# Second projections of a decoder layer: own values of kv heads 0 and 1 first, context values of these heads made between the others

## The chip, the cores and the metric

The kernel runs on one core of a Trainium2 chip. Its time is the device time of one execution in microseconds (us), given as the median of several runs. The kernel before takes 2528.96 us (three runs, 2527.68 to 2529.01). The engines are named as in the profile: PE is the matrix engine (PEld its weight loads), DVE the vector engine, ACT the scalar engine, POOL the GpSimd engine, and SP the queue that issues the DMAs.

## What is computed

One decoder layer, in float32, on x of 8 sequences x 100 tokens x 1024 and a context of 8 x 722 x 1024. Each of the three parts is added to its input and followed by a layer norm:

```python
x = layernorm(x + retention(x))                     # 8 heads, decay matrix, gate
x = layernorm(x + cross_and_self_attention(x, ctx)) # 16 query heads, 4 kv heads of 128
x = layernorm(x + swiglu(x))                        # 1024 -> 4096 -> 1024
```

The change is in the second part:

```python
q, k, v = x @ wq, x @ wk, x @ wv           # q: 16 heads, k and v: 4 heads ("own" keys and values)
q, k = rope(rms_norm(q, qw)), rope(rms_norm(k, kw))
k_ctx, v_ctx = rms_norm(ctx @ wk_ctx, kw), ctx @ wv_ctx
k_full, v_full = concat(k_ctx, k), concat(v_ctx, v)      # 722 + 100 rows
out = softmax(q @ k_full.T / sqrt(128) + mask) @ v_full  # per head
y = out @ wo
```

## The kernel before

**Arithmetic.** All large products are made from operands split in a high and a low part, so each 128x128 block of a product is three matmuls (`mm3`, lines 86, 87, 88). A weight block of 1024x128 is loaded by `load_w` (line 76) into one of three `wst` buffers and split by ACT (line 67) and DVE (line 68) into one of four `w` buffers. Context weights have been split earlier and are read whole by `load_ws` (line 82). `proj` makes one product of a weight block with 400 tokens (one half of the batch) or with half of a context: 24 matmuls into one PSUM bank. Banks are handed out in turn under three tags: three of "a", four of "s", one of "v". A bank is free for its next use when ACT and DVE have read it.

**Order.** The program is written stage by stage, but the instructions of each engine are put in an order by a scheduler that goes by its own estimate of when things become ready. Each engine works its own list strictly in that order. SP's list of DMAs is in order too: a DMA that waits holds those behind it. Tiles lie in pools; when a pool is closed its memory is used again by the next pool, and an instruction that writes there waits for the last reader of the tiles that lay there (`reuse_waits="tile"`).

**The stages around the change.**

1. `out_proj` (line 239 adds the residual) and the layer norm end the first part. They leave the normed activations in four tiles `z`, two for each half of the batch.
2. *Second projections* (pool "l2"). For each kv head there are six blocks: four query heads, one own key, one own value. Each block is made for both halves of the batch, so there are 48 "half-blocks". A query or key half-block takes the squares (ACT), a sum over partitions on POOL (line 125), the rotation (lines 133 to 137), an inverse root (lines 113 to 120), the scaling (line 645), a split, and a store to DRAM. A value half-block is only copied, transposed on PE (line 148), split into the single buffer `vs` and stored (line 637). Blocks come in groups: the four queries of kv head 0, its key and value, and then two by two. The context of the first sequence is loaded beside them, and the context keys of kv heads 0 and 1 (`context_keys`) are made between groups.
3. *Attention* (pools "cx" and "c1"), for 8 sequences x 4 kv heads, which are called heads below. Each makes context keys (unless made before) and context values (`context_values`, line 613), transposes the values (line 677), takes seven blocks of scores (lines 707, 711, 712), the maximum over partitions (line 125), the exponentials (line 730), their sum (line 733), the product with the values into the "v" bank, and the division by the sum (lines 747 to 752). The result goes through `ofs` and the split pair `oh` to DRAM (line 755).
4. `out_proj` of the second part, with the pool "y2" for its sum `y` and residual `rs`. Its first group makes four blocks at once: three in the "a" banks and one in an "s" bank, 48 matmuls each. The fifth block takes the first "a" bank again.

In the kernel before, pool "y2" is opened ahead of the attention, so its memory is apart from that of "cx" and "c1".

Of the kernel before, what the change touches and what calls it, by code (L numbers as in the profile page):

```python
# [16 lines left out]
P = 128  # L17
B, T, D = 8, 100, 1024
NB = 4
# [20 lines left out]
def decoder_layer(ctx, tc, xT, cT, w1, wo1, w2, wo2, wc, w3, wd, gw, qw, kw, trig, dec, mask, out):  # L40
# [15 lines left out]
    def f32(ap):  # L56
        return ap.bitcast(F32)
# [8 lines left out]
    def split2(hi, lo, src):  # L66
        nc.scalar.copy(hi, src)  # L67
        nc.vector.tensor_tensor(lo, src, f32(hi), ALU.subtract)  # L68

    def load_w(src, w=None, parts=1):  # L70
        st = wp.tile([P, KT * P], F32, tag="wst", name="wst", bufs=3)
        if w is None:
            w = wp.tile([P, 2, KT * P], FR, tag="w", name="w", bufs=4)
        for i in range(parts):
            c = slice(i * KT * P // parts, (i + 1) * KT * P // parts)
            nc.sync.dma_start(out=st[:, c], in_=src[:, c])
            split(w[:, :, c], st[:, c])
        return w
# [17 lines left out]
    def acc_tag():  # L96
        turn[0] += 1
        return "as"[turn[0] % 2]

    def proj(w, z, n=N, tag="a"):  # L100
        acc = bank(tag)[:, :n]
        for k in range(KT):
            t = z[k // QT]
            mmw(acc, w, k, t[:, 0, k % QT, :n], t[:, 1, k % QT, :n], k == 0, k == KT - 1)
        return acc
# [4 lines left out]
    def inv_root(pool, ss, eps, n=N, pin=False):  # L110

        r = pool.tile([P, n], F32, tag="r0", name="r0")
        ln = nc.scalar.activation(r, ss, AF.Ln, bias=eps)
        if pin:
            tc.keep_in_program_order(ln)
        nc.scalar.activation(r, r, AF.Exp, scale=-0.5)
        q = pool.tile([P, n], F32, tag="r1", name="r1")
        nc.scalar.activation(q, r, AF.Square)  # L118
        nc.vector.scalar_tensor_tensor(q, ss, eps, q, ALU.add, ALU.mult)  # L119
        nc.vector.scalar_tensor_tensor(q, q, 3.0, r, ALU.subtract, ALU.mult)  # L120
        return q

    def all_red(pool, x, tag, op=RED.add):
        y = pool.tile([P, N], F32, tag=tag, name=tag)
        nc.gpsimd.partition_all_reduce(y, x, P, op)  # L125
        return y

    def rope(pool, acc, cosw, sinw, tag="t1", op=ALU.add):

        t1 = pool.tile([P, N], F32, tag=tag, name=tag)  # L130
        t2 = pool.tile([P, N], F32, tag="t2", name="t2")
        h = P // 2
        nc.scalar.copy(t2[0:h], acc[h:P])
        nc.scalar.copy(t2[h:P], acc[0:h])
        nc.vector.tensor_tensor(bt(t1), bt(acc), cosw[:, None, :].to_broadcast([P, NB, T]), ALU.mult)
        nc.vector.tensor_tensor(bt(t2), bt(t2), sinw[:, None, :].to_broadcast([P, NB, T]), ALU.mult)
        nc.vector.tensor_tensor(t1, t1, t2, op)
        return t1

    def tokens_first(pool, acc, copied=True):  # L140

        vt = acc
        if copied:
            vt = pool.tile([P, N], F32, tag="vt", name="vt", bufs=1)
            nc.scalar.copy(vt, acc)
        tr = bank("s")
        for b in range(NB):
            nc.tensor.transpose(tr[0:T, b * P:(b + 1) * P], vt[:, b * T:(b + 1) * T], ident)  # L148
        return tr[0:T]
# [424 lines left out]
    def load_context(b):  # L574

        cz.clear()
        for hf in range(2):
            n = SN[hf]
            z = [big([P, 2, QT, SH]) for _ in range(2)]
            for k in range(0, KT, 2):  # L580
                cs = wp.tile([P, KT * P], F32, tag="wst", name="cs", bufs=3)
                cs = cs[:, :2 * n].rearrange("p (k n) -> p k n", k=2)
                nc.sync.dma_start(out=cs, in_=cT[b, :, k:k + 2, hf * SH:hf * SH + n])
                split(z[k // QT][:, :, k % QT:k % QT + 2, :n], cs)
            cz.append(z)

    def context_keys(kv):

        kall = ka.tile([P, 2, SC + T], FR, tag="kall", name="kall")
        wk = load_ws(2 * kv)  # L590
        sq = ka.tile([P, SC], F32, tag="ksq", name="ksq", bufs=1)
        ss = ka.tile([P, 6 * P], F32, tag="kss", name="kss", bufs=1)
        row = dr.tile([6, P], F32, tag="row", name="row", bufs=2)
        nc.gpsimd.memset(ss[:, SC:], 1.0)

        def step(hf):
            n, at = SN[hf], slice(hf * SH, hf * SH + SN[hf])
            acc = proj(wk, cz[hf], n)
            nc.scalar.activation(sq[:, at], acc, AF.Square)  # L599
            nc.gpsimd.partition_all_reduce(ss[:, at], sq[:, at], P, RED.add)  # L600
            nc.scalar.activation(kall[:, 0, at], acc, AF.Copy, scale=kws)
            nc.vector.scalar_tensor_tensor(kall[:, 1, at], acc, kws, f32(kall[:, 0, at]), ALU.mult, ALU.subtract)
            if hf:
                nc.sync.dma_start(out=row.rearrange("c p -> (c p)")[None, :], in_=ss[0:1])
        return step, (kall, row)

    def context_values(kv):

        wv = load_ws(2 * kv + 1)
        vt = ka.tile([P, SC], F32, bufs=1, tag="cvt", name="cvt")  # L610
        for hf in range(2):
            copy = nc.scalar.copy if hf == 0 else nc.vector.tensor_copy
            copy(vt[:, hf * SH:hf * SH + SN[hf]], proj(wv, cz[hf], SN[hf]))
        return vt


    early = []
    with sbuf("l2", 2) as p:
        for kv in range(NKV):
            for i0, i1 in ((0, 4), (4, 6)) if kv == 0 else ((0, 2), (2, 4), (4, 6)):  # L620
                if (kv, i0) == (0, 4):
                    load_context(0)
                ws = [load_w(w2[kv, i]) for i in range(i0, i1)]
                if (kv, i0) in ((1, 2), (2, 2)):
                    step, kept = context_keys(kv - 1)
                    early.append(kept)
                if (kv, i0) in ((1, 2), (2, 0), (2, 2), (3, 0)):
                    step(i0 == 0)
                for half in range(2):
                    bs = slice(half * NB, (half + 1) * NB)  # L630
                    for i in range(i0, i1):
                        acc = proj(ws[i - i0], z1[half], tag=acc_tag())
                        if i == 5:
                            tr = tokens_first(p, acc).rearrange("p (b d) -> p b d", b=NB)
                            vs = p.tile([T, NB, 2, P], FR, tag="vs", name="vs", bufs=1)
                            split2(vs[:, :, 0], vs[:, :, 1], tr)
                            nc.sync.dma_start(out=f32(vd[kv, :, bs]), in_=f32(vs))
                            continue
                        sq = p.tile([P, N], F32, tag="sq", name="sq")
                        nc.scalar.activation(sq, acc, AF.Square)  # L640
                        ss = all_red(p, sq, "ss")
                        tb = tq if i < 4 else tk
                        t = rope(p, acc, tb[:, 0], tb[:, 1])
                        r = inv_root(p, ss, eps_k)
                        nc.vector.scalar_tensor_tensor(
                            t, t, -0.5 if i < 4 else -0.5 * math.sqrt(P), r, ALU.mult, ALU.mult)
                        d = p.tile([P, NB, 2, T], FR, tag="d", name="d", bufs=3)
                        split2(d[:, :, 0], d[:, :, 1], bt(t))
                        nc.sync.dma_start(out=f32(qd[kv, i, :, bs] if i < 4 else kd[kv, :, bs]), in_=f32(d))
    z1pool.__exit__(None, None, None)  # L650


    y2pool = sbuf("y2", 1)
    y2p = y2pool.__enter__()
    with sbuf("cx", 2) as p, sbuf("c1", 1) as p1:
        for b in range(B):
            if b > 0:
                load_context(b)
            for kv in range(NKV):
                if early:  # L660
                    kall, row = early.pop(0)
                else:
                    step, (kall, row) = context_keys(kv)
                    step(0)
                    step(1)
                nc.sync.dma_start(out=f32(kall[:, :, SC:]), in_=f32(kd[kv, :, b]))
                vall = p.tile([P, NC, 2, P], FR, tag="vall", name="vall")
                nc.sync.dma_start(out=f32(vall[C5:P, 5]), in_=f32(vd[kv, 0:P - C5, b]))
# [1 line left out]
                q = p.tile([P, 4, 2, T], FR, tag="q", name="q")  # L670
                nc.sync.dma_start(out=f32(q).rearrange("p h l t -> p h (l t)"),
                                  in_=f32(qd[kv, :, :, b]).rearrange("h p l t -> p h (l t)"))
                vt = context_values(kv)
                for c0, c1, rows in ((0, 3, P), (3, 5, P), (5, 6, C5)):
                    tr = bank("s")
                    for c in range(c0, c1):
# [91 lines left out]

    fp = ctx.enter_context(sbuf("fp", 1, "right"))
    z2p = ctx.enter_context(sbuf("z2", 1, "right"))
    zb = {}
# [273 lines left out]
```

## Time and profile before

| | |
|---|---|
| median of three runs | 2528.96 us |
| the profiled execution, its own time | 2527.58 us |
| its span, first to last instruction | 2525.8 us |
| mean granted PE clock | 0.994 of full speed |
| busy: PE, DVE, ACT, POOL | 98%, 79%, 54%, 18% of the span |
| second projections, up to the last own value | about 590 to 841 us of the span |
| attention | about 849 to 1642 us |

What is worked out from single rows belongs to the profiled execution of 2527.58 us, which lies 1.38 us under the median. A row of the grouped view reads: line, engine, operation, output<-inputs, shape, count | busy time, mean length of one in ns | idle time of the engine just before it, and what ended that. A row of the waits reads: the waiting engine, output and line <- what it waited for: total us, times, longest. A window row reads: from:to, length, and for each engine busy us (number of instructions), then the granted PE clock, the DMA share, and GB/s.

### The profile page before, as it was taken

To read this page: it belongs to the slowest core of one execution; us is meant where nothing else is said; L and a number is where in the kernel's file an instruction comes from. 1 tells how busy PE (TensorE), PEld (TensorE's weight loads), DVE (VectorE), ACT (ScalarE), POOL (GpSimd) and SP (SyncE) were. 2 spreads that over 40 slices of the span, in tenths; PEclk is the share of its full clock that TensorE was granted. 3 is DMA by queue.
4 is the path that set the end of the run, shared out by engine and by line. 5 is a ranking of instruction groups with operands and counts; after the bars stand their busy time and mean duration, and the time that the engine had idled before them with its cause. 6 is when DMAs were issued, how large, how long until landed. Compare 5 with 4: busy or idle time off the path is not lost.

```text
span 2525.8 us, 37215 instructions
## 1 busy us (share of the span) xinstructions
PE 2478.2 (98%) x14042; PEld 2440.9 (97%) x14042; DVE 2000.6 (79%) x3106; ACT 1353.7 (54%) x2272; POOL 466.8 (18%) x230
## 2 busy tenths in 40 slices
PE   8999999999999999999999999999999999999997
PEld 8999999998899999999999999999999999998996
DVE  7778876568989798998998998866988777666756
ACT  6666676336667466655656566533554454432222
POOL 0111111002555243433433434100000000000000
PEclk9999999999999999999999999999999999999999
DMA  7333445774444654455554554575455445388742
GB/s 239 110 110 127 136 146 186 240 268 147 143 147 147 202 174 156 151 170 161 163 165 146 163 190 125 199 259 162 137 183 195 163 158 167 127 298 313 249 135 86
DMA packets 232898, 438.16 MB, mean 173 GB/s; under 512 B 47594, under 2 KB 176490, under 8 KB 220302
## 3 DMA queue, kind: packets, MB, share of 16 engines
q1 hardware_dynamic: 231566, 431.59, 51.3%
q0 software_dynamic: 1152, 4.19, 1.1%
q8 instruction: 110, 1.80, 0.3%
q14 instruction: 70, 0.57, 0.1%
HBM read 326.38 MB, written 109.35 MB: 173 GB/s over the span
## 4 chain that ended last, share of the span: by engine, by line
PE 89%; DVE 6%; issue 2%; DMA 1%; ACT 1%; SPq 0%; DVEq 0%; ACTq 0%
PE a L88 18%; PE a L86 18%; PE a L87 17%; PE s L88 9%; PE s L87 9%; PE s L86 9%; PE v L86 2%; PE v L88 2%; PE v L87 2%; PE s L486 1%; PE s L677 1%; DVE r L120 1%; DVE r L119 1%; PE s L148 1%; DVE d L68 1%
## 5 line engine op out<-in xcount | busy, mean ns | idle before, releaser
L86 PE MATMUL a<-big,w 128*128 128x400 f32 (+2 forms) x1824 | 616.3, 339 | 10.5 <-ACT big L67 7.1
L87 PE MATMUL a<-big,w 128*128 128x400 f32 (+2 forms) x1824 | 615.7, 338 | 0.0
L88 PE MATMUL a<-big,w 128*128 128x400 f32 (+2 forms) x1824 | 614.4, 338 | 0.0
L67 ACT CAST w<-wst 128x1024 fp32r<-128x1024 f32 (+1 forms) x243 | 251.8, 1039 | 431.0 <-PE s L88 152.3
L68 DVE TENSOR_TENSOR w<-wst,w 128x1024 fp32r<-128x1024 f32 (+1 forms) x243 | 297.7, 1227 | 120.2 <-ACT w L67 119.0
L86 PEld LDWEIGHTS a<-big,w 128*128 128x128 f32 x1824 | 343.7, 189 | 12.3 <-ACT big L67 7.4
L87 PEld LDWEIGHTS a<-big,w 128*128 128x128 f32 x1824 | 344.5, 189 | 1.4 <-DVE big L68 0.3
L88 PEld LDWEIGHTS a<-big,w 128*128 128x128 f32 x1824 | 344.2, 189 | 1.0 <-DVE w L68 0.3
L86 PE MATMUL s<-big,w 128*128 128x400 f32 x680 | 236.0, 347 | 0.1
L87 PE MATMUL s<-big,w 128*128 128x400 f32 x680 | 234.7, 345 | 0.0
L88 PE MATMUL s<-big,w 128*128 128x400 f32 x680 | 234.6, 346 | 0.0
L125 POOL PARTITION_ALL_REDUCE ss<-sq x56 | 159.4, 2851 | 337.4 <-DMA zd<-y 166.9
L600 POOL PARTITION_ALL_REDUCE kss<-ksq x64 | 162.3, 2536 | 138.7 <-ACT ksq L599 136.9
L86 PE MATMUL a<-z,w 128*128 128x400 f32 x504 | 174.5, 346 | 8.2 <-ACT r L118 4.3
L88 PE MATMUL a<-z,w 128*128 128x400 f32 x504 | 174.9, 347 | 0.7 <-DVE w L68 0.7
L87 PE MATMUL a<-z,w 128*128 128x400 f32 x504 | 175.0, 347 | 0.0
L87 PE MATMUL s<-z,w 128*128 128x400 f32 x416 | 144.5, 347 | 2.3 <-DVE z L68 2.3
L86 PE MATMUL s<-z,w 128*128 128x400 f32 x416 | 145.2, 349 | 0.0
L88 PE MATMUL s<-z,w 128*128 128x400 f32 x416 | 145.1, 349 | 0.0
L711 ACT ACTIVATE s<-s,rk 128x400 f32<-128x400 f32 x160 | 88.3, 591 | 97.0 <-DVE sm L733 65.0
L86 PEld LDWEIGHTS s<-big,w 128*128 128x128 f32 x680 | 127.6, 188 | 1.4 <-ACT w L67 0.4
L87 PEld LDWEIGHTS s<-big,w 128*128 128x128 f32 x680 | 127.6, 188 | 1.1
(274 smaller groups left out, 5562.6 us busy)
## 6 DMA issues: line engine op xcount, KB each, us to landing
wst<-in_w SPq DMA_DIRECT2D x135, 512.0 KB
w<-wcd SPq DMA_DIRECT2D x64, 1024.0 KB
wst<-in_wo SPq DMA_DIRECT2D x64, 512.0 KB
wst<-in_wd SPq DMA_DIRECT2D x80, 256.0 KB
hd<-h SPq DMA_DIRECT2D x12, 1400.0 KB
big<-o1d SPq DMA_DIRECT2D x16, 800.0 KB
qd<-d SPq DMA_DIRECT2D x32, 400.0 KB
q<-qd SPq DMA_DIRECT2D x32, 400.0 KB
```

Of the source, the lines that this page charges most:

```text
L67: nc.scalar.copy(hi, src)
L68: nc.vector.tensor_tensor(lo, src, f32(hi), ALU.subtract)
L86: nc.tensor.matmul(acc, lh, rh, start=start, stop=False, skip_group_check=chain)
L87: nc.tensor.matmul(acc, lh, rl, start=False, stop=False, skip_group_check=chain)
L88: nc.tensor.matmul(acc, ll, rh, start=False, stop=stop, skip_group_check=chain)
L119: nc.vector.scalar_tensor_tensor(q, ss, eps, q, ALU.add, ALU.mult)
L120: nc.vector.scalar_tensor_tensor(q, q, 3.0, r, ALU.subtract, ALU.mult)
L125: nc.gpsimd.partition_all_reduce(y, x, P, op)
L148: nc.tensor.transpose(tr[0:T, b * P:(b + 1) * P], vt[:, b * T:(b + 1) * T], ident)
L486: nc.tensor.matmul(bt(o)[:, b], vv[:, b * P:(b + 1) * P], pf[:, b], start=True, stop=True)
L600: nc.gpsimd.partition_all_reduce(ss[:, at], sq[:, at], P, RED.add)
L711: nc.scalar.activation(sc, sp, AF.Copy, scale=rk[:, c:c + 1])
```

## The change

The list of groups is written out. The first group now holds the own values of kv heads 0 and 1 and two queries of head 0. Then come the other two queries of head 0, the two keys of heads 0 and 1, the queries of heads 1 and 2, key and value of head 2, and head 3. Beside context keys 0 and 1, the context values of kv heads 0 and 1 of the first sequence are made between these groups; the order is values 0, keys 0, values 1, keys 1, each over two groups. `context_values` gets two buffers for its result `cvt` in place of one. For kv head 2 the context keys lie in a buffer of pool "c1", so that three buffers `kall` are in use. Pool "y2" is opened after the attention instead of before it. The work of each block is the same.

```diff
-    def context_keys(kv):
+    def context_keys(kv, pool=None):
 
-        kall = ka.tile([P, 2, SC + T], FR, tag="kall", name="kall")
+        kall = (pool or ka).tile([P, 2, SC + T], FR, tag="kall", name="kall", bufs=1 if pool else 2)
...
     def context_values(kv):
 
         wv = load_ws(2 * kv + 1)
-        vt = ka.tile([P, SC], F32, bufs=1, tag="cvt", name="cvt")
-        for hf in range(2):
+        vt = ka.tile([P, SC], F32, bufs=2, tag="cvt", name="cvt")
+
+        def step(hf):
             copy = nc.scalar.copy if hf == 0 else nc.vector.tensor_copy
             copy(vt[:, hf * SH:hf * SH + SN[hf]], proj(wv, cz[hf], SN[hf]))
-        return vt
-    early = []
+        return step, vt
+
+    def context(make, *args):
+        if early[make]:
+            return early[make].pop(0)
+        step, kept = make(*args)
+        step(0)
+        step(1)
+        return kept
+
+    early = {context_keys: [], context_values: []}
     with sbuf("l2", 2) as p:
-        for kv in range(NKV):
-            for i0, i1 in ((0, 4), (4, 6)) if kv == 0 else ((0, 2), (2, 4), (4, 6)):
-                if (kv, i0) == (0, 4):
-                    load_context(0)
-                ws = [load_w(w2[kv, i]) for i in range(i0, i1)]
-                if (kv, i0) in ((1, 2), (2, 2)):
-                    step, kept = context_keys(kv - 1)
-                    early.append(kept)
-                if (kv, i0) in ((1, 2), (2, 0), (2, 2), (3, 0)):
-                    step(i0 == 0)
-                for half in range(2):
-                    bs = slice(half * NB, (half + 1) * NB)
-                    for i in range(i0, i1):
-                        acc = proj(ws[i - i0], z1[half], tag=acc_tag())
...
+        groups = [[(0, 5), (1, 5), (0, 0), (0, 1)], [(0, 2), (0, 3)], [(0, 4), (1, 4)], [(1, 0), (1, 1)], [(1, 2), (1, 3)],
+                  [(2, 0), (2, 1)], [(2, 2), (2, 3)], [(2, 4), (2, 5)], [(3, 0), (3, 1)], [(3, 2), (3, 3)], [(3, 4), (3, 5)]]
+        steps = {2: (context_values, 0), 4: (context_keys, 0), 6: (context_values, 1), 8: (context_keys, 1)}
+        for g, blocks in enumerate(groups):
+            ws = [load_w(w2[kv, i]) for kv, i in blocks]
+            if g == 0:
+                load_context(0)
+            if g in steps:
+                make, kv = steps[g]
+                step, kept = make(kv)
+                early[make].append(kept)
+            if g >= 2 and g - g % 2 in steps:
+                step(g % 2)
+            for half in range(2):
+                bs = slice(half * NB, (half + 1) * NB)
+                for (kv, i), w in zip(blocks, ws):
+                    acc = proj(w, z1[half], tag=acc_tag())
...
-    y2pool = sbuf("y2", 1)
-    y2p = y2pool.__enter__()
     with sbuf("cx", 2) as p, sbuf("c1", 1) as p1:
...
-                if early:
-                    kall, row = early.pop(0)
-                else:
-                    step, (kall, row) = context_keys(kv)
-                    step(0)
-                    step(1)
+                kall, row = context(context_keys, kv, p1 if kv == 2 else None)
...
-                vt = context_values(kv)
+                vt = context(context_values, kv)
...
+    y2pool = sbuf("y2", 1)
+    y2p = y2pool.__enter__()
     fp = ctx.enter_context(sbuf("fp", 1, "right"))
```

More of the change, by code (lines that the diff above doesn't have):

```diff
@@ L609, in context_values @@
         wv = load_ws(2 * kv + 1)
-        vt = ka.tile([P, SC], F32, bufs=1, tag="cvt", name="cvt")
-        for hf in range(2):
+        vt = ka.tile([P, SC], F32, bufs=2, tag="cvt", name="cvt")
+        def step(hf):
             copy = nc.scalar.copy if hf == 0 else nc.vector.tensor_copy
             copy(vt[:, hf * SH:hf * SH + SN[hf]], proj(wv, cz[hf], SN[hf]))
-        return vt
-    early = []
-    with sbuf("l2", 2) as p:
-        for kv in range(NKV):
-            for i0, i1 in ((0, 4), (4, 6)) if kv == 0 else ((0, 2), (2, 4), (4, 6)):
-                if (kv, i0) == (0, 4):
-                    load_context(0)
-                ws = [load_w(w2[kv, i]) for i in range(i0, i1)]
-                if (kv, i0) in ((1, 2), (2, 2)):
-                    step, kept = context_keys(kv - 1)
-                    early.append(kept)
-                if (kv, i0) in ((1, 2), (2, 0), (2, 2), (3, 0)):
-                    step(i0 == 0)
-                for half in range(2):
-                    bs = slice(half * NB, (half + 1) * NB)
-                    for i in range(i0, i1):
-                        acc = proj(ws[i - i0], z1[half], tag=acc_tag())
[L633 to L649, printed above, removed]
@@ new lines, in context_values @@
+        return step, vt
[7 more added lines that the diff above has]
+    early = {context_keys: [], context_values: []}
+    with sbuf("l2", 2) as p:
+        groups = [[(0, 5), (1, 5), (0, 0), (0, 1)], [(0, 2), (0, 3)], [(0, 4), (1, 4)], [(1, 0), (1, 1)], [(1, 2), (1, 3)],
[15 more added lines that the diff above has]
+                    acc = proj(w, z1[half], tag=acc_tag())
+                    if i == 5:
+                        tr = tokens_first(p, acc).rearrange("p (b d) -> p b d", b=NB)
+                        vs = p.tile([T, NB, 2, P], FR, tag="vs", name="vs", bufs=1)
+                        split2(vs[:, :, 0], vs[:, :, 1], tr)
+                        nc.sync.dma_start(out=f32(vd[kv, :, bs]), in_=f32(vs))
+                        continue
+                    sq = p.tile([P, N], F32, tag="sq", name="sq")
+                    nc.scalar.activation(sq, acc, AF.Square)
+                    ss = all_red(p, sq, "ss")
+                    tb = tq if i < 4 else tk
+                    t = rope(p, acc, tb[:, 0], tb[:, 1])
+                    r = inv_root(p, ss, eps_k)
+                    nc.vector.scalar_tensor_tensor(
+                        t, t, -0.5 if i < 4 else -0.5 * math.sqrt(P), r, ALU.mult, ALU.mult)
+                    d = p.tile([P, NB, 2, T], FR, tag="d", name="d", bufs=3)
+                    split2(d[:, :, 0], d[:, :, 1], bt(t))
+                    nc.sync.dma_start(out=f32(qd[kv, i, :, bs] if i < 4 else kd[kv, :, bs]), in_=f32(d))
```

## The prediction

> **What bounds the kernel now.** I began with busy shares and windows.
>
> ```profile
> PE 2478.2 (98%) x14042; PEld 2440.9 (97%) x14042; DVE 2000.6 (79%) x3106; ACT 1353.7 (54%) x2272; POOL 466.8 (18%) x230
> ```
> ```profile
> 600.00:720.00 120.00, 105.69 (x543) 103.23 (x542) 116.65 (x166) 84.44 (x163) 61.97 (x20) 0.93 0.43 143
> 720.00:840.00 120.00, 119.25 (x667) 118.44 (x665) 110.27 (x157) 85.47 (x164) 62.70 (x25) 1.00 0.46 155
> 1620.00:1640.00 20.00, 20.00 (x109) 19.61 (x108) 15.50 (x22) 9.64 (x13) 3.13 (x2) 1.00 0.49 150
> ```
>
> PE bounds the whole. Only in the first half of the second projections does it fall back: 543 matmuls in 120 us against 667 in the next 120. At 0.18 us each, **22.3 us** are lost, while DVE is busy 116.65 of 120. The third row is the attention's end: PE is full there (109 matmuls of 400 columns in 20 us). Next, PE's waits from 560 to 960:
>
> ```profile
> PE a L86 <- ACT r L118: 4.3, 1, 4.3
> PE s L148 <- ACT vt L145: 4.1, 3, 2.8
> PE a L86 <- ACT w L67: 2.7, 2, 1.6
> PE s L87 <- DVE z L68: 2.3, 1, 2.3
> PE a L86 <- DMA w<-wcd: 2.1, 1, 2.1
> PE s L677 <- ACT cvt L613: 0.8, 1, 0.8
> ```
>
> In the timeline the 4.3 us wait ends at 634.85. It is the tenth half-block, waiting for the bank of the fourth, which DVE first reads at 634.14. DVE began the queries only at 610.67, after the second half's norm and split, when PE had finished four query half-blocks. Matmuls after that wait start every 0.33 us until 639.3, then every 0.18: about 2.1 us more. DVE's groups from 720 to 840:
>
> ```profile
> L120 DVE SCALAR_TENSOR_TENSOR r<-r,r 128x400 f32<-128x400 f32 x20 | 20.2, 1008 | 0.1
> L645 DVE SCALAR_TENSOR_TENSOR t<-t,r 128x400 f32<-128x400 f32 x20 | 19.1, 955 | 0.2
> L136 DVE TENSOR_TENSOR t<-t,tq 128x400 f32<-128x400 f32 x16 | 13.3, 831 | 1.9 <-ACT t L134 1.9
> L68 DVE TENSOR_TENSOR d<-t,d 128x400 fp32r<-128x400 f32 x20 | 12.9, 647 | 0.9 <-ACT d L67 0.6
> L68 DVE TENSOR_TENSOR w<-wst,w 128x1024 fp32r<-128x1024 f32 x10 | 12.9, 1295 | 0.7 <-ACT w L67 0.6
> L119 DVE SCALAR_TENSOR_TENSOR r<-ss,eps_k,r 128x400 f32<-128x400 f32 x20 | 12.5, 626 | 0.0
> ```
>
> With lines 135 to 137 complete, the seven operations of a query or key half-block sum to 103.2 us for 20. All groups sum to 120.6 but occupy 110.27 (neighbours overlap), so one costs 103.2 x 110.27/120.6 / 20 = **4.7 us of DVE** against 24 x 0.181 = 4.35 of PE. A value half-block costs DVE 0.68, a weight block about 1.25.
>
> **The Trainium skill.** "SBUF — State Buffer", section "SBUF: two separate sides", says that DVE and GpSimd share a port pair under an exclusive lock. The trace agrees: DVE operations of 0.56 us take 2.1 when they start inside a POOL reduction (at 628.98, 663.57, 678.21). "TensorE: Matmul & The Clock Gate", Part 1, has the array run at half clock after an idle window; here 0.33 against 0.18 us after 4.3 us idle. "PSUM — Partial Sum Buffer", "Engine vs sequencer instructions", calls the ACT, DVE and POOL queues strict FIFO; every idle row here fits.
>
> **The change, part by part.** I compared the two programs' instruction orders.
>
> *(a) Values first.* Two of the four weights that meet half 0 early are now values, so at 610.7 DVE owes one query half-block, not four. But PE makes only three half-blocks before it needs half 1's activations: it arrives at 600.4 instead of 604.8 and waits for the same z (607.4). **Cost 4.4 us.** The four `vs` writes follow closely through one buffer: ACT waits for `vd<-vs` each time (5 to 7 us from issue to release, at 719 and 840), with the queries' squares behind it on ACT and their first DVE reads behind those. I count about 7 us and then 5 us of DVE idleness up to 641. Two transposes wait for their copies in turn: **1.4 us**. In SP's order two of these stores stand ahead of a weight load each; that load is for a later group, so I count nothing, at worst one wait of 2 us.
>
> *(b) Context values between the groups.* Four times 24 matmuls of 0.166 us (16 us) move from attention to projections: zero by themselves, since PE does them either way. The two 1 MB weight reads move along on SP; one may land late as the key weights did (2.1). They give DVE time: two query groups with one context block cost DVE 8 x 4.7 + 4 x 1.25 + 0.5 = 43.1, PE 8 x 4.35 + 8 = 42.8. DVE thus does not catch up in those groups, only at key and value of head 2 (35 against 43).
>
> *(c) What is recovered.* Of the waits above, all but the z wait and its slow matmuls may go: 4.3+2.1, 2.1+2.0 (slow matmuls after it), 1.6+0.7, 2.8+2.0, 0.6+0.8 (the other two transposes), 0.8 = **19.8 us**. Following bank by bank with the 12 us of DVE idleness, I find PE close to the six-half-block lead that the banks allow, around 661 to 700, and new waits of 2 to 9 us; I take 5.5. Net: 19.8 - 4.4 - 1.4 - 5.5 = **8.5 us gained** (2 to 14; not more, since the z wait stays).
>
> *(d) Pool "y2" after the attention.* This is no mere bookkeeping. `y` and `rs` now lie where attention tiles lay. In DVE's order before, the residual add (line 239) of the first `out_proj` block stands in the middle of the last heads (at 1615.0). In the new order all of these adds follow the last head's `oh`, and the first `rs` load stands in SP's queue behind the store of that `oh`. The three "a" banks stay full until then, and PE's next work after the last head's values is the fifth block, which needs the first "a" bank. **PE has nothing else**; its order is fixed. The chain, from these rows of the groups:
>
> ```profile
> L125 POOL PARTITION_ALL_REDUCE mb<-sm x32 | 83.3, 2603 | 217.9 <-DVE sm L733 217.9
> ...
> L749 DVE TENSOR_TENSOR mb<-mb,r 128x400 f32<-128x400 f32 x32 | 21.8, 680 | 16.5 <-ACT r L748 16.5
> ...
> L750 DVE SCALAR_TENSOR_TENSOR r<-mb,r 128x400 f32<-128x400 f32 x32 | 18.2, 568 | 0.1
> ...
> L752 DVE SCALAR_TENSOR_TENSOR ofs<-v,r 128x400 f32<-128x400 f32 x32 | 18.1, 565 | 0.0
> ...
> L748 ACT ACTIVATE r<-r 128x400 f32<-128x400 f32 x32 | 17.2, 537 | 0.8
> ...
> L747 ACT ACTIVATE r<-mb 128x400 f32<-128x400 f32 x32 | 17.1, 535 | 24.1 <-POOL mb L125 24.1
> ...
> L67 ACT CAST oh<-ofs 128x400 fp32r<-128x400 f32 x32 | 17.0, 531 | 22.5 <-DVE ofs L752 22.5
> ```
>
> After the last `sm`: reduction 2.6, two ACT steps 1.1, three DVE steps 1.8, `oh` 0.5 + 0.6, two SP issues 0.7, landing of a 200 KB load about 2.4 (`tp<-in_xT` at 19.56), the add 0.6, hand-overs 0.7: 11.0 us. PE ends its values at about the last `sm`, so it idles **11 us**, then runs slow: **2.1**.
>
> Ahead of it, PE has only the 48 matmuls of the "s" block (8.7 us) between the last scores and the values, where it had 82 (15 us). A split of `w` that needs the end of this block now stands inside the last head's exponentials, on ACT and on DVE. From that end: cast 1.1, split 1.2, three `pl` and two sums 4.3, last matmuls 1.1, hand-overs 0.4: values end 8.1 us after it, where 3.8 would do. **Cost 4.3.** Sum of (d): 17.4 us, bounded by 12 (the load lands at once, exponentials early) and 20.
>
> *(e) The third `kall` and second `cvt`* cost nothing that I can name: key production is hidden under PE-bound attention, and two more buffers can only loosen it; if the memory of "cx" comes free late, the first scores wait, up to 3 us, kept in the range.
>
> **Sum:** -8.5 + 17.4 = +8.9. Against the profiled execution's 2527.6 this gives 2536.5. That execution lies 1.4 under the median, so beside the runs: **2538 us**.
>
> **Rivals.** *Draw* (not slower): DVE idles under 5 us at the start, so the projections lose nothing but the z wait, and the tail costs its lower bound: -14 + 12 to 14, 2527 to 2529. For it: DVE had caught up by 720, where ACT and DVE wait for PE. Against: the single `vs` buffer. It decides if the second `vs` cast waits under 3 us. *Tail hidden*, the change then faster: something fills PE while the first adds are held; 2520. Against: fixed order, three "a" banks. *Values stall*: ACT's waits for `vd<-vs` take more than six half-blocks of lead and PE idles with slow matmuls in the first groups too, eating the gain: 2529 + 17 = 2546 or more. *The change doesn't do what it says* is excluded by the orders: values stand first and the context values are moved.
>
> **How the numbers follow.** A measurement of this kernel can tell about 0.2%, 5 us, from no change. Forecast (net +4 to +14) 0.66, draw 0.15, tail hidden 0.07, values stall 0.12. The forecast's lowest sliver (+4 to +5) counts as no change, as does most of the draw; its fastest part does not. Slower 0.76, same 0.15, faster 0.09. The range 2528 to 2546 leaves out the hidden tail and the worst of the stalls.
>
> **What would show it.** Right: in the last head, the add of line 239 after `oh`, PE idle 10 us or more after the last "v" matmul and waiting for DVE `y` L239, half-rate matmuls behind it; in 600 to 720, about 590 matmuls; context values near 660; the last scores 4 to 8 us earlier than 1617.9. Wrong: no PE wait near the end of attention (then d fails), or PE waits from 610 to 720 above 10 us (then c fails).

## The result, and the profile after

The changed kernel takes **2566.24 us** (median of four runs, 2561.51 to 2570.29), against 2528.32 for the kernel before beside it: 1.0151 times, interval 1.0139 to 1.0163. It is slower by 37.9 us, where 8.9 was forecast. Its profiled execution took 2561.51 us, the least of the four, with a span of 2559.7; against the span of before, 2525.8, that is 33.9 us more. The other 4.0 us are spread between runs: those of this kernel lie within 9 us, those of before within 1.5. No single trace shows why.

The page's line of busy time, then the windows that answer to those of before, and two at the new end of the attention:

```profile
PE 2488.7 (97%) x14042; PEld 2448.4 (96%) x14042; DVE 2012.2 (79%) x3106; ACT 1347.6 (53%) x2272; POOL 485.7 (19%) x230
```
```profile
600.00:720.00 120.00, 107.66 (x577) 105.94 (x576) 102.18 (x148) 78.78 (x152) 53.11 (x19) 0.94 0.44 148
720.00:840.00 120.00, 115.24 (x640) 114.82 (x639) 109.37 (x154) 81.87 (x157) 60.88 (x25) 0.99 0.43 144
...
1640.00:1660.00 20.00, 13.81 (x55) 12.11 (x53) 14.42 (x22) 9.16 (x14) 4.45 (x2) 0.83 0.26 88
1660.00:1680.00 20.00, 14.92 (x67) 14.86 (x68) 7.93 (x12) 2.59 (x3) 0.00 (x0) 0.74 0.40 119
```

The first half of the second projections gained: 577 matmuls where before had 543 (590 were forecast). The second half lost nearly as much, 640 against 667. The end of the attention, full before, now has two thin windows. PE's waits from 580 to 1720 us say what is behind this:

```profile
PE a L86 <- DMA w<-wcd: 8.4, 2, 4.8
PE a L86 <- DVE y L239: 7.7, 1, 7.7
PE a L86 <- ACT z L67: 4.0, 1, 4.0
PE a L86 <- ACT cvt L614: 3.8, 3, 2.2
PE v L86 <- ACT ph L67: 2.7, 1, 2.7
PE a L87 <- DVE z L68: 2.6, 1, 2.6
PE a L86 <- DMA big<-o2d: 2.4, 1, 2.4
PE s L86 <- DMA q<-qd: 1.9, 1, 1.9
```

Of the waits of before for `r` (4.3 us) 0.5 is left, of those for `vt` (4.1) 1.8. In their place stand two late reads of context weights, `w<-wcd`. The wait for `y` of line 239 is the one that step (d) named. The rows for `cvt` (3.3 of its 3.8 us) and `big<-o2d` stand inside the attention, where before had no wait from 900 us on. The tail itself, in PE's timeline and then in DVE's (start, length, instruction, and in brackets the idle time before it):

```profile
1657.02 0.41 PE L88 MATMUL v<-ph,vall 128*128 128x400 f32 x1
1665.08 0.70 PE L86 MATMUL a<-big,w 128*128 128x400 f32 x1 [7.65 <-DVE y L239]
```
```profile
1660.52 0.58 DVE L68 TENSOR_TENSOR oh<-ofs,oh 128x400 fp32r<-128x400 f32 x1 [0.59 <-ACT oh L67]
1664.45 1.06 DVE L239 TENSOR_TENSOR y<-a,rs 128x400 f32<-128x400 f32 x2 [3.36 <-DMA rs<-zd]
```

This is the chain of step (d), link by link: `oh` at 1660.52, then the load of `rs`, then the add, and only then PE's next block.

**Where the 34 us lie.** Idle rows alone are too little, since PE also runs slowly after many of them. So I took, from the starts of all 14042 matmuls, the lag of a kernel behind the kernel before at equal work: the time of a mark, less that of the same mark before, less the matmuls that one has done more than the other, at 0.181 us for 400 columns. The length of a matmul of each kind is taken as proportional to its columns, so a figure is good to about 1 us. The marks are the first "v" matmul of head 0; the end of the matmul just ahead of the first "v" matmul of head 31, so that a wait for that head's exponentials counts to the tail; and the last matmul of the program. A column is the lag added between two marks.

| kernel | ratio to before, interval | to head 0 | in the attention | tail |
|---|---|---|---|---|
| changed kernel | 1.0151 (1.0139 to 1.0163) | 3.9 | 12.3 | 17.8 |
| x1, before with late y2 | 1.0074 (1.0059 to 1.0089) | 2.6 | 0.3 | 15.6 |
| x2, no third kall | 1.0139 (1.0122 to 1.0156) | 4.3 | 19.3 | 15.4 |
| x3, and y2 early | 1.0096 (1.0081 to 1.0111) | 6.1 | 14.7 | 0.0 |
| x4, context weights first | 1.0166 (1.0146 to 1.0186) | 8.3 | 23.9 | 16.9 |
| y1, list of groups alone | 1.0045 (1.0033 to 1.0058) | 7.8 | 0.2 | 0.0 |
| y2, second cvt alone | 1.0016 (1.0010 to 1.0023) | 1.7 | 0.9 | -0.6 |
| y3, early values alone | 1.0092 (1.0078 to 1.0106) | 8.5 | 13.6 | 2.4 |
| y4, list and one early value | 1.0099 (1.0084 to 1.0115) | 6.8 | 20.9 | -0.4 |
| z2, one own value last | 1.0009 (1.0003 to 1.0016) | 0.4 | 0.0 | 2.3 |
| z3, one own value first | 1.0016 (1.0009 to 1.0022) | 1.2 | 0.0 | 2.4 |
| v2, accumulated weights | 1.0036 (1.0022 to 1.0051) | 7.1 | 0.0 | 0.0 |

The ratios come from all executions of a kernel, the lags from its profiled one. That lies within 5 us of the kernel's median, but for x4, where it lies 10 us above. The small tails of y2, y3, y4, z2 and z3 arise only from about 2330 us on, long after the attention. z1, w1 and v1 work on other queries and keys; only their second projections are read.

### The profile page after: what moved, and what is told of

Read it like the earlier page. It is cut to its first block, busy times and chain, and to the rows that moved or that the text cites. A ratio compares the mean times of both kernels' runs of the same rounds, so it can differ in the third digit from the quotient of the medians.

```text
span 2559.7 us, 37251 instructions
## 1 busy us (share of the span) xinstructions
PE 2488.7 (97%) x14042; PEld 2448.4 (96%) x14042; DVE 2012.2 (79%) x3106; ACT 1347.6 (53%) x2272; POOL 485.7 (19%) x230
## 4 chain that ended last, share of the span: by engine, by line
PE 78%; DVE 9%; DMA 5%; ACT 3%; issue 3%; POOL 2%; SPq 0%; POOLq 0%; DVEq 0%; ACTq 0%
PE a L86 15%; PE a L88 15%; PE a L87 15%; PE s L88 9%; PE s L87 8%; PE s L86 8%; PE v L86 1%; DMA rr<-row 1%; PE s L486 1%; PE v L88 1%; PE v L87 1%; DVE r L120 1%; DMA row<-kss 1%; POOL kss L600 1%; DVE r L119 1%
## 5 line engine op out<-in xcount | busy, mean ns | idle before, releaser
L600 POOL PARTITION_ALL_REDUCE kss<-ksq x64 | 185.8, 2908 | 274.8 <-ACT ksq L599 274.8
L125 POOL PARTITION_ALL_REDUCE ss<-sq x56 | 154.2, 2760 | 358.8 <-ACT sq L653 246.5
```

## Experiments

**The tail.** x1 is the kernel before with one move:

```diff
-    y2pool = sbuf("y2", 1)
-    y2p = y2pool.__enter__()
     with sbuf("cx", 2) as p, sbuf("c1", 1) as p1:
...
+    y2pool = sbuf("y2", 1)
+    y2p = y2pool.__enter__()
     fp = ctx.enter_context(sbuf("fp", 1, "right"))
```

> The kernel before with pool "y2" opened after the attention, and nothing else. Theory (step (d) holds by itself): the last head ends as in the changed kernel, PE waits 7 to 11 us for DVE y L239, and the whole is 13 to 17 us above the kernel before (2541 to 2546), with the middle of the attention as before (within 3 us at head 30). Rival 1: the 16 us that the changed kernel loses inside the attention also come from the pool, since other memory gives the scheduler another order; then about 30 us above before (2558). Rival 2: the tail's loss needs the later arrival at the last head; then under 5 us above before.

It took 2545.26 us against 2527.22: 18.0 more, 1 above the expected 13 to 17. The attention is as before to within 0.3 us, the tail loses 15.6. (The other 2.6 us fall ahead of head 0, where the scheduler's order differs a little too.) From 1600 to 1720 us PE's first row of waits is

```profile
PE a L86 <- DVE y L239: 10.8, 1, 10.8
```

So the move of the pool, alone, costs about what step (d) said, and neither rival holds. From the other side come x2 and x3. x2 is the changed kernel without the third `kall`; x3 is x2 with the pool opened ahead of the attention again.

```diff
-                kall, row = context(context_keys, kv, p1 if kv == 2 else None)
+                kall, row = context(context_keys, kv)
```

The rest is in x3 alone; `mix` is then taken from `mixp`:

```diff
+    y2pool = sbuf("y2", 1)
+    y2p = y2pool.__enter__()
     with sbuf("cx", 2) as p, sbuf("c1", 1) as p1:
...
-    y2pool = sbuf("y2", 1)
-    y2p = y2pool.__enter__()
+    mixpool = sbuf("mix", 1)
+    mixp = mixpool.__enter__()
```

> The changed kernel without the third kall buffer (kv head 2 takes it from the same two as the others). Theory (the third buffer lets key production be placed ahead of the softmax work that frees banks and ACT, and that costs the 16 us inside the attention): 12 to 16 us below the changed kernel, about 2552, the loss at head 31 falling from 19 to 3 to 7 us, the tail's wait for DVE y L239 kept. Rival (the loss comes from early values, the second cvt buffer or the late pool y2): within 4 us of the changed kernel.

> As the kernel without the third kall, and with y and rs in a pool opened ahead of the attention again (only the tile mix, used later, keeps a late pool, since the memory holds no more). Theory (step (d)): 13 to 17 us below the same kernel with the late pool, no wait of PE for DVE y L239 at the last head. Rival (the attention's losses are the pool's): 25 us below or more. Rival (mix's late pool takes over the wait): within 5 us.

x2 took 2563.87 us. Its interval overlaps that of the changed kernel, and its attention loses no less (19.3), so the third `kall` is not what costs: the theory on it fell. x3 took 2551.51, 12.4 under x2, where 13 to 17 was expected; its tail is down from 15.4 to 0.0, and the row for `y` L239 is gone. That 14.7 us are still lost in the attention says that those are not the pool's either.

**The attention.** Three kernels split the rest of the change. y1 is the kernel before with the new list of groups alone. y2 is the kernel before with `bufs=2` for `cvt` alone. y3 is the kernel before with its old list, the early context values and two `cvt` (y2 and y3 keep the tile `mix` in a late pool for space). Against the changed kernel (y1, y3) and the kernel before (y2), with the pool early and two `kall` in y1 and y3:

```diff
# y1
-        steps = {2: (context_values, 0), 4: (context_keys, 0), 6: (context_values, 1), 8: (context_keys, 1)}
+        steps = {4: (context_keys, 0), 6: (context_keys, 1)}
...
-            if g >= 2 and g - g % 2 in steps:
-                step(g % 2)
+            if g in (4, 5, 6, 8):
+                step(g in (5, 8))
# y2
-        vt = ka.tile([P, SC], F32, bufs=1, tag="cvt", name="cvt")
+        vt = ka.tile([P, SC], F32, bufs=2, tag="cvt", name="cvt")
# y3
-        groups = [[(0, 5), (1, 5), (0, 0), (0, 1)], [(0, 2), (0, 3)], [(0, 4), (1, 4)], [(1, 0), (1, 1)], [(1, 2), (1, 3)],
+        groups = [[(0, 0), (0, 1), (0, 2), (0, 3)], [(0, 4), (0, 5)], [(1, 0), (1, 1)], [(1, 2), (1, 3)], [(1, 4), (1, 5)],
```

> The kernel before with the new list of groups alone: own values of heads 0 and 1 first, context keys 0 and 1 between the same query blocks as before, no early context values, one cvt buffer, y2 ahead of the attention. PE's order in the attention is the one of before, block for block. Theory (the list itself recovers about 19 us of PE's losses between 620 and 840 and pays about 9 for z and two transposes; what ate the rest were the two late reads that belong to the early values): 2516 to 2521, thus 6 to 11 below the kernel before, and no PE loss inside the attention. Rival (values first costs as much as it brings, through vs and a DVE that still lags): 2524 to 2534.

> The kernel before with a second cvt buffer and nothing made earlier (tile mix in a late pool for space). PE's order in the attention differs from that of before in the first six heads and is the same from then on. Theory (the loss inside the attention comes from the order in which production of the next heads is laced into the heads, not from the buffer): PE loses under 5 us in the attention, all of it before head 8, and the whole is within 6 us of the kernel before. Rival (a second buffer lets ACT and DVE fall behind everywhere): 10 us or more lost in the attention, spread to the end.

> The kernel before with its old list of groups (four queries of head 0 first), and the context values of heads 0 and 1 made early in the same groups 3 to 10 as the changed kernel has them, two cvt buffers, mix in a late pool; y2 ahead of the attention. PE's order in the attention falls into another cycle than that of before. Theory (early values alone set the attention's phase and cost it 10 to 13 us): 10 to 16 us lost inside the attention, 2538 to 2548 in all. Rival (the loss belongs to the list of groups): under 4 us lost inside the attention, 2525 to 2533 in all.

In the attention y1 loses 0.2 us, y2 0.9, y3 13.6, close to the 12.3 of the changed kernel. **The early context values cost it;** the list, the second `cvt`, the third `kall` and the pool do not. (y3 also makes context keys one or two groups later, as the changed kernel does; no run has that alone.) Each early value takes 48 matmuls, half of the context blocks that a head has as independent work between its scores, out of heads 0 and 1. The scheduler fills the place with blocks of later heads and thereby starts on another pattern, in which blocks of keys and values are laced between scores and products. In the kernel before this pattern repeats every four heads from head 1 on. y1 has it too, and y2 joins it after the first few heads; the changed kernel and y3 run in others to the end. y4 tests whether the pattern is to blame, since it changes from one to the other on its way. Its change to the list of y1 is one entry, and with it one half of context keys 1 comes one group earlier:

```diff
-        steps = {4: (context_keys, 0), 6: (context_keys, 1)}
+        steps = {2: (context_values, 0), 4: (context_keys, 0), 6: (context_keys, 1)}
```

> The new list of groups, with the context values of head 0 alone made early (one cvt buffer, so no second one), y2 ahead of the attention. PE's order laces the heads as the early-values kernels do up to about head 17 and from there on exactly as the kernel before. Theory (the order of the lacing costs the time): PE loses 4 to 8 us between heads 0 and 17 and under 1.5 from 17 to 31; 2522 to 2532 in all. Rival (DVE and ACT are simply too full, whatever the order, once PE enters the attention with them behind): the loss goes on evenly after head 17. Rival (the second cvt buffer is what costs): no loss in the attention at all.

Windows of y4 over heads 1 to 18 and over the later ones, and PE's main row of waits from 900 to 1320 us:

```profile
900.00:1320.00 420.00, 409.48 (x2384) 396.78 (x2383) 370.21 (x634) 241.47 (x472) 160.18 (x83) 0.98 0.47 155
1320.00:1620.00 300.00, 300.00 (x1784) 293.22 (x1783) 270.91 (x471) 179.90 (x345) 114.40 (x60) 1.00 0.52 171
```
```profile
PE a L86 <- DVE kall L602: 7.8, 5, 2.1
```

It loses 20.8 us up to head 17 and 0.1 from there to head 31, where its order is that of before and PE is full (300.00 of 300). DVE is as busy in one part as in the other (88% and 90%). So not DVE's load but the order decides: five times PE stands at an "a" block whose bank still awaits DVE's part of `kall`, 7.8 us in all, with matmuls at half rate behind three of them. The size was more than twice the 4 to 8 expected, so the whole, 2552.43 us, lies far above the expected 2522 to 2532. In the changed kernel the 12.3 us go mostly in other rows (`cvt`, `big<-o2d`), each once or twice, so each pattern has margins of its own. Why the scheduler holds these patterns for as good is not shown. y3 lost 8.5 us ahead of the attention too: at 638 PE stands 11.0 us for DVE's first reading of a query's bank, where before it stood 4.3. Why DVE comes to it so late is not shown either.

**The second projections.** y1, which has neither early values nor a late pool, is still 11.4 us slower (2538.57 against 2527.13): the list loses 7.8 us up to head 0, where I had expected a gain; even the rival's range ended at 2534. (y1 also loads the first context one group earlier than before, as the changed kernel does.) Its PE waits 13.4 us for two reads `w<-wcd` of context keys. In the changed kernel the second of its two late reads stands so in SP's timeline:

```profile
742.67 4.77 SPq L662 DMA_DIRECT2D qd<-d  x2
747.53 0.38 SPq L82 DMA_DIRECT2D w<-wcd  x1
```

Two stores of queries that wait for DVE's `d` are ahead of it in SP's list. SP's own waits from 690 to 765 us are led by them:

```profile
SPq L662 <- DVE d L68: 37.6, 10, 7.0
```

PE needs the read at 748.1; it uses it from 753.0 on. x4 lets the program ask for each such read ahead of its group's weights; z1 sends another tile in the stores, so that SP waits for no `d`.

```diff
+            if g in steps:
+                make, kv = steps[g]
+                step, kept = make(kv)
+                early[make].append(kept)
             ws = [load_w(w2[kv, i]) for kv, i in blocks]
...
-            if g in steps:
-                make, kv = steps[g]
-                step, kept = make(kv)
-                early[make].append(kept)
```

> The changed kernel with each read of a context weight pair (w from wcd) issued by the program ahead of its group's own weight loads instead of after them. Theory (the two reads came late, 8.4 us of PE waits with about 4 us at half rate behind them, because they stood in SP's queue behind stores that wait for DVE): the waits for w from wcd fall under 2 us and the time falls by 8 to 13 us, to about 2555. Rival (DVE lags anyway and PE only waits elsewhere, for banks): the waits go to DVE or ACT rows of the projections and the time stays within 4 us.

```diff
-                    nc.sync.dma_start(out=..., in_=f32(d))
+                    nc.sync.dma_start(out=..., in_=tq[:, None].to_broadcast([P, NB, 2, T]))
```

> The changed kernel, where the stores of queries and own keys (qd, kd) send the rotation table tq instead of d, so that SP need not wait for DVE's d; the attention then works on other queries and keys, and its order differs. PE's order in the second projections is the one of the changed kernel. Only the time up to 850 us is read. Theory (the reads w from wcd are late because SP's list holds them behind stores that wait for a lagging DVE): PE's waits for w from wcd fall from 8.4 to under 2.5 us, and PE loses 5 to 9 us less between 690 and 760 (12.0 in the changed kernel). Rival (the buffer of w comes free too late for a read of 5.5 us, whatever SP does): the waits stay above 6 us.

In z1 the first read is in time, and the second, which now follows a weight load, 1.4 us late. So the stores ahead made 7.0 of the 8.4 us. Yet PE gains nothing. By the count of matmuls, which stand in one order in the changed kernel and z1 and in nearly that order in x4, it loses 13.6 us from the first late read to the last own value in the changed kernel, 15.1 in z1 (whose stage lies 29 us later, behind other waits) and 19.2 in x4 (whose profiled execution is its longest). PE's waits in x4 from 620 to 850, and in z1 from 700 to 850:

```profile
PE s L148 <- ACT vt L145: 5.0, 1, 5.0
PE a L88 <- DVE w L68: 4.7, 4, 1.7
```
```profile
PE s L148 <- ACT vt L145: 3.4, 1, 3.4
PE a L86 <- DVE cvt L614: 2.7, 1, 2.7
```

PE comes earlier to the own value of head 2 and waits there for ACT's copy `vt`, which in ACT's list stands behind casts `d` that wait for DVE. The rival to x4 held: 2566.51 us, within 0.3 of the changed kernel. I then took DVE's sum of work for the bound of the stage, and three kernels tested it. In w1 ACT fills `d`'s low part, with a copy of the high part, in DVE's place; v1 does this and what z1 does; v2 is the kernel before with the low parts of the second projections' weights made by ACT and an accumulating DMA.

```diff
# w1
-                    split2(d[:, :, 0], d[:, :, 1], bt(t))
+                    nc.scalar.copy(d[:, :, 0], bt(t))
+                    nc.scalar.copy(d[:, :, 1], bt(t))
# v2
+    def load_wa(src):
...
+        nc.scalar.copy(w[:, 0], st)
+        nc.scalar.activation(w[:, 1], f32(w[:, 0]), AF.Copy, scale=-1.0)
+        nc.gpsimd.dma_start(out=f32(w)[:, 1], in_=st, accum_op=ALU.add)
...
-                ws = [load_w(w2[kv, i]) for i in range(i0, i1)]
+                ws = [load_wa(w2[kv, i]) for i in range(i0, i1)]
```

> The changed kernel, where ACT writes the high part of d into its low part too, in place of DVE's subtraction: the low parts of queries and own keys are wrong, DVE does 40 x 0.65 = 26 us less in the second projections and ACT 40 x 0.53 = 21 us more (it was busy 167 of 250). PE's order in the projections stays nearly the same. Only the time up to 850 us is read. Theory (DVE's sum of work bounds the second projections, so PE loses about the same whichever way the blocks are ordered, and a wait taken away comes back elsewhere): PE loses under 5 us between 620 and 850 (14.4 in the changed kernel), with its waits for w from wcd under 3 us. Rival (single waits by their order and buffers, not DVE's sum): 10 us or more stay, among them a wait of over 5 us for w from wcd or for a transposed value.

> The changed kernel with both: the stores of queries and own keys send the table tq instead of d, and ACT writes d's low part (as a copy of the high part) instead of DVE, so the queries and keys are wrong. Only PE's time in the second projections is read, from the first late read of w on. Theory (two bounds in series: SP's list holds the reads, and once these are early DVE's backlog holds ACT's copy of the own value): PE loses under 5 us from there to the end of the stage, where it lost 11.9 in the changed kernel, 12.8 with constant stores alone and 15.5 with less DVE work alone. Rival (neither; the order of ACT's list by itself): 8 us or more stay, at the transposition of the own value of head 2.

> The kernel before, where the low part of each weight block of the second projections is made as minus the high part by ACT and an accumulating DMA that adds the block, as the kernel does for the context weights, instead of by DVE's subtraction: DVE does 24 x 1.29 = 31 us less in that stage, ACT 24 x 1.05 = 25 us more, and POOL issues 24 DMAs more. Theory (DVE's sum bounds the stage of the kernel before): PE loses 8 to 18 us less between 620 and 840 (22.3 before), 2510 to 2520 in all. Rival (the weights now come later by a DMA's landing, and ACT's list is the longer one): PE waits for w and the time is 2527 to 2545.

**What the theory foretold came in none of the three.** (The 11.9, 12.8 and 15.5 us that the expectation of v1 names are sums at the waits alone; over the whole stretch they are 13.6, 15.1 and 16.4.) w1 has DVE at 192.18 of the 230 us from 620 to 850 (209.54 in the changed kernel), and PE still loses 17.2 us there, where the changed kernel lost 14.4; its reads `w<-wcd` are late by 7.0, behind stores that now wait for ACT. v1 loses 16.3 us over the stretch, 8.6 of it at the own value of head 2 and 5.2 at a context block that waits 3.4 us for DVE's `r` L119. v2 took 2535.07 us, in the range of its rival: PE now waits for `w`, whose low part comes by DMA. But although its DVE is busy only 210 of the 250 us from 600 (230 before), PE also waits at the same block as before:

```profile
PE a L97 <- DMA w<-wst: 4.9, 2, 4.4
PE a L95 <- DVE t L144: 4.8, 1, 4.8
```

Line 144 there is line 135, the first reading of a query's bank, and the wait is that of 4.3 us before. So taking work from DVE and giving it to ACT does not bring PE forward. All three kernels do both: ACT is busy 174 of 230 us in w1 (159 in the changed kernel), 192 of 250 in v2 (174 before). Less work on DVE with none added on ACT is untested. What is left as an explanation, argued and not shown, is the place of each half-block's steps in the lists of ACT, DVE and POOL, each waiting for another. Which position would have to move is left open.

**One own value only.** z2 and z3 swap one query of the first group for one own value, last or first in the group.

```diff
-        [(0, 0), (0, 1), (0, 2), (0, 3)], [(0, 4), (0, 5)], ...
+        [(0, 0), (0, 1), (0, 2), (0, 5)], [(0, 3), (0, 4)], ...
```

> The kernel before with one swap in its list of groups: the first group makes queries 0, 1, 2 of head 0 and then its own value, the second group query 3 and the key. Nothing else; attention and tail keep the order of before. Theory (DVE owes one half-block less by 635, so PE's wait of 4.3 us for the bank of the fourth query with its 2.1 us at half rate goes, and the arrival at z is as before): PE loses 4 to 9 us less by 840, 2518 to 2524 in all. Rival (the wait moves to a later transposition or a read of w from wcd): 2526 to 2531.

> As the kernel with one value in the first group, but the value first, ahead of queries 0, 1, 2. Theory (PE's loss at z in the changed kernel, 14.6 us by 620 against 6.8, comes from having values at the head of the group, which changes what PE can do before z of the second half is there): 3 to 8 us lost more by 620 than with the value last, 2523 to 2530 in all. Rival (the loss at z comes from having two values there): the same loss by 620 as with the value last, within 1.5 us.

Both are within 0.2% of before, 2530.16 and 2531.27 us against 2527.49. By 620 us both have lost 10.1 (6.8 before, 14.6 in the changed kernel). The equal sums hide different waits, though. PE's waits from 590 to 620, in z2 and then in z3:

```profile
PE s L148 <- ACT vt L145: 4.0, 1, 4.0
PE a L87 <- DVE z L68: 0.8, 2, 0.5
```
```profile
PE a L87 <- DVE z L68: 2.9, 1, 2.9
PE a L86 <- ACT z L67: 1.8, 1, 1.8
```

With the value first, PE waits 4.7 us for `z`, as the changed kernel does with two values (6.6); with the value last it hardly waits for `z`, but 4.0 us to transpose the value. So a value at the head does cost at `z`, as the theory of z3 had it, though its sum did not come; the equal sums of the rival came by chance. For z2 the rival held: the wait of before at 635 did go, but by 850 it has lost 31.5 us against 30.7: it waits 6.0 us for DVE's `t` ahead of the context keys, at 674.63. No kernel of the study beats the kernel before.

## Why the prediction was wrong

The direction was right, and step (d), on which it rested, held. The size was missed by 25 us of span (8.9 against 33.9), in two places of about 12 us each: the second projections, step (c), and the attention, steps (b) and (e).

**Step (d), right.** 17.4 us were forecast; 15.6 came in x1 alone and 17.8 in the changed kernel, and the 15.4 of x2 go when the pool is put back (x3). The parts shifted: PE idles 10.8 us in x1 as forecast (11), but 7.65 in the changed kernel, as its last product itself ran at half rate after a wait of 2.7 us for `ph`, while DVE's chain went on.

**Step (c), wrong in the size of the new waits, with (a) too low.** Up to 620 us I forecast 5.8 us more lost (4.4 + 1.4) and 7.8 came: the arrival at `z` cost 12.0 us where before lost 4.1, since the matmuls after the two waits run slowly until 612.4, which I had not priced. From 620 to 850 I forecast 14.3 us less (19.8 less 5.5). The losses named did go, down to 2.5 of the 23.9 of before. But the new ones were 11.9 and not 5.5, so 9.5 was won. Nearly all of the 11.9 are the two reads of context weights, 5.5 and 6.4 with their slow matmuls. I had named them in step (b) and given one of them 2.1 us, that of the key weights of before, without counting what stands ahead of them in SP's list and how late DVE is there. From 850 to 900 I forecast nothing and 5.1 came, mostly the first scores' wait for `q<-qd`, 1.9 us with slow matmuls, whose load is issued at 860.49 behind the last stores of `d`. In all +3.4 where -8.5 was forecast. The idleness of DVE was nearer: 12 us forecast up to 641, 16.3 came from 600 to 641, 7.1 of it for `vs`. That it comes to bear as a read held in SP's list, I did not see. Even so, the two reads are not all of it: with them in time, z1 and x4 lost as much elsewhere, and what bounds the stage stays open. PE's waits from 610 to 720 were 5.7 us, under the 10 named as the sign that (c) fails; the longer of the two reads came later.

**Steps (b) and (e), wrong by 12.3 us.** "Zero by themselves, since PE does them either way" overlooks that the blocks are what fills PE between scores. y3 and y4 show the cost of the other order; y1, y2, x1 and x2 that the list, `cvt`, the pool and `kall` do not have it. I had compared the two orders around the edit and at the end, and not over the 32 heads between, where the difference is plain. The last scores came 19.1 us later than before (1637.0) and not 4 to 8 earlier.

**The rivals.** Of *values stall* the size was about right for the projections (no gain at all; +3.4 by 900), its place was not: behind `z` the first groups ran almost without a stall (1.6 us for a transposition, 0.5 for `r`), and the loss came at the reads. *Draw* and *tail hidden* needed a cheap tail. None of the cases had a loss inside the attention beyond the 3 us of step (e), so the range ended at 2546.

## What to carry over

Where a scheduler lays out fixed lists, compare the whole order after an edit, not its surroundings: work that only fills gaps sets the pattern of a later stage, and a steady stage that had PE full can lose 12 us and more without any operation having changed. For each transfer that is moved, write down what stands ahead of it on its queue and what that waits for, and only then its length. And a wait that is taken away in a stage where three engines wait for each other in turn is won only if the next one is not there already: here 21 us went and over half came back.

## What the runs showed of the hardware

Slow matmuls after an idle PE could be as dear as the idleness itself where waits were short or came in pairs. In the changed kernel a wait of 1.1 us (at 1149.8) cost 1.5 in all, one of 2.2 (at 1049.0) cost 4.3. A gap of 3.8 us from one matmul's due start to the next one's start cost 5.5, one of 4.9 cost 6.4, one of 8.4 (in y1) cost 10.3; two gaps at `z`, 4.2 and 3.1 us with one matmul between them, cost 12.0. In y4 the five waits for `kall`, 7.8 us, and some smaller ones made a loss of 20.8. A read of 1 MB of context weights took 5.5 us from its issue to PE's first use (698.06 to 703.59, and 747.53 to 753.03), as long as 30 matmuls of 400 columns; asked for that late, behind two stores, it could not be in time. The runs of the changed kernel, of x2 and of x4 lie 8 to 11 us apart, those of x1, x3, y1, y3, y4, z2 and z3 3 to 6; why is not shown.
